# The first expert layer of a two-block kernel, cut into two half passes with other work beside each

## The chip, the cores and the metric

The kernel runs on one core of a Trainium2 chip, as one launch. The metric is the device time of a launch in microseconds (us). Five engines work side by side, each with its own queue of instructions: PE (TensorE, matrix multiplications and transposes), DVE (VectorE), ACT (ScalarE), POOL (GpSimd) and SP (SyncE, which here only starts transfers). The page calls a loading of stationary operands for a matmul PEld. Transfers between the chip's main memory and its on-chip memory are DMAs, carried by 16 DMA engines. Instructions of different engines wait for each other through semaphores; within one engine they run in the order in which they stand.

## The reference

The input is x, 4 batches of 512 tokens with 256 features, and a context of 4 batches of 1601 rows with 256 features. All arithmetic is in 32-bit floating point. Four blocks follow each other, and each adds its result to x:

```
x = x + attention_0(context, layernorm(x))   # 8 heads of 128, keys from the context and the tokens
x = x + experts_0(layernorm(x))              # 8 experts, 2 per token, limited room
x = x + attention_1(context, x)              # 8 heads of 32, queries from x, keys from the context
x = x + experts_1(layernorm(x))              # 8 experts, 2 per token, no limit
```

The change concerns the second block and the borders around it. A router gives each of the 2048 tokens a softmax over 8 experts, of which the two largest are taken. Each expert has room for 512 entries (the capacity is 2 x 2048 / 8). Entries are numbered in the order of the tokens, so that batch 0 fills the first places of every expert, then batch 1 and so on; an entry beyond 512 is dropped. Expert e computes, for its 512 places,

```
h = gelu(xb[e] @ w1[e])      # 512 x 256 by 256 x 1024, gelu in its tanh form
y = h @ w2[e]                # 512 x 1024 by 1024 x 256
```

and a token adds its two results, each multiplied by its softmax weight, and a bias. The third block then computes queries from the layernormed tokens, keys and values from the context, and a softmax with the row maximum taken away.

## The kernel before

**Stages.** The kernel has four parts after each other. The first attention handles 4 batches x 8 heads x 4 tiles of 128 queries; in its tail TensorE multiplies weights with values (`ps_o`, L829) and DVE adds the projected tile to x (L850). Each tile's weights pass through transfers (`swapped<-attn`) and a transpose on DVE (L821), and these transfers stand in SP's and ACT's queues. The routing of a batch (`route`) runs inside the attention of the next batch; only the last batch's is left for the second part. Instructions outside the parts with a written order are placed by a scheduler that goes by dependences and buffers; inside `in_order(...)` they stand as the program lists them. The second attention is such a part, from its first maxima on.

**Routing.** `route` gives three steps. `normalize` makes the layernorm `xn` of the batch and lets POOL add the bias to x. `choose` transposes `xn` (L163), multiplies by the router's weights (`ps_l`, L246), and DVE works out the two experts of each token and, with two small matmuls (`ps_c`, L285 and L288), each token's place, written as integers to `slot` (L298). A running count per expert is kept in `taken`. `send` lets POOL scatter the rows of `xn` to their places in a table in main memory, `slot_x` (L304), eight scatters of 128 rows.

**Experts.** `w_next` is the pair of weight matrices loaded ahead (L978, L979, one megabyte each). For each expert, SP loads its 512 rows from `slot_x` (`sx`, L1101), TensorE transposes them (L163), `expert` makes the hidden layer in blocks of 128 x 512 (L1041) with gelu on ACT (L1083), and `results` of the expert before multiplies by the second weights (L1054, blocks of 128 x 256), copies on DVE (L1088) and writes to `slot_y` in main memory (L1089). Between the experts SP issues up to six of 41 row clears (L385): transfers that fill two tables of the fourth block with zeros and a mark, about 540 KB each.

**Keys and values.** `keys_values(b)` loads the transposed context of batch b (L991), and makes keys (`ps_k1`, L1000) and values (`ps_v1`, L1016) of the second attention. ACT and DVE take turns to copy the results out (L109, L111). Those of batches 0 and 1 are made in the second part, before the experts: keys(0) beside the last batch's routing, keys(1) beside its scatters.

**Into the second attention.** POOL gathers the results of batch 0 from `slot_y` (L323, eight gathers), DVE adds them to x (L340), then follow a layernorm and transposes, the queries (`ps_q`, L1162), and per unit of 256 queries and 4 heads the scores (`ps_s`, L1216), their maxima on DVE (L1227, seven steps of two reductions), `negated` (L1236) and `to_row` (L1249, L1253). `keyed` is a table whose rows are filled with a constant (L1143, ACT, whole) and then loaded with the keys (L1182). `asked` takes queries and maxima (L1192). The weights (`ps_w`, L1266) of unit 0 follow.

The lines of the expert loop around which the order turns:

```
        normalize()
        kvs = [run(keys_values(ps_h, "h", 0))]
        choose()
        send()
        kvs.append(run(keys_values(ps_h, "h", 1)))
```

Of the kernel before, what the change touches and what calls it, by code (L numbers as in the profile page):

```python
# [43 lines left out]
CT = CAP // P  # L44
# [25 lines left out]
def xattn_ffn_twice(ctx: ExitStack, tc: tile.TileContext, a: dict, out: bass.AP):  # L70
# [143 lines left out]
    nc.vector.memset(taken, 0.0)  # L214
    prob = [const.tile([P, NX], F32, name=f"prob{k}") for k in range(2)]
# [4 lines left out]
    def route(b, rt, psum, tag):  # L220


        xn = rt.tile([P, NT, D], F32, tag="xn", name="xn")
# [16 lines left out]
        def choose():  # L240
            xnT = rt.tile([P, DC, S], F32, tag="xnT", name="xnT")
# [38 lines left out]
            for t in range(NT):  # L280
                nc.vector.tensor_copy(earlier[:, t, :], taken)
                nc.vector.tensor_tensor(taken, taken, cnt[:, t, :], ALU.add)
            ps = psum.tile([P, NT, E], F32, tag=tag, name="ps_c")
# [258 lines left out]
    with ExitStack() as st:  # L542
        w = st.enter_context(tc.tile_pool(name="a_w", bufs=1))
        one = st.enter_context(tc.tile_pool(name="a_one", bufs=1))
        rt = st.enter_context(tc.tile_pool(name="a_rt", bufs=1))
# [15 lines left out]
        kvin = one.tile([P, DC, NB, 4, 32], F32, name="kvin")  # L561
# [7 lines left out]
        def load_ctx(b):  # L569
            t = one.tile([P, NM, D], F32, tag="ctx", name="ctx_b")  # L570
            full = (NM - 1) * P
            nc.sync.dma_start(
                t[:, : NM - 1, :], a["ctx"][b, :full, :].rearrange("(t p) d -> p t d", p=P)
            )
            nc.sync.dma_start(t[:TAIL, NM - 1, :], a["ctx"][b, full:, :])
            return t
# [3 lines left out]
        wo = w.tile([P, H0, D], F32, name="wo")  # L580
# [3 lines left out]
        ctx_b = one.tile([P, NM, D], F32, tag="ctx", name="ctx_b")  # L584
# [27 lines left out]
        def keys_input(b, ctx_b):  # L612
# [9 lines left out]
            def latents():  # L622
                state["lat"] = lat = one.tile([P, NT, D], F32, tag="lat", name="lat")
                layernorm(two, lat, x[b], NT)
# [253 lines left out]
        scrap = one.tile([P, NT, D], F32, tag="lat", name="scrap")  # L878
# [15 lines left out]
        for n in range(n_steps + 4):  # L894
            b, h, t = n // (H0 * NT), n // NT % H0, n % NT
            if n < n_steps:
# [26 lines left out]
                if h == 1 and t == 1 and b > 0:  # L923
                    for k, f in enumerate(route(b - 1, rt, ps_t, "t")):
                        later[n + k].append(f)
# [109 lines left out]
    def expert(psum, pool, xT, w1, act):  # L1035

        hT = pool.tile([P, FC, 512], F32, tag="hT", name="hT")
        for f in range(FC):
            ps = psum.tile([P, 512], F32, tag="h", name="ps_h")
            for c in range(DC):  # L1040
                nc.tensor.matmul(  # L1041
                    ps,
                    lhsT=w1[:, c, f * P : (f + 1) * P],
                    rhs=xT[:, c, :],
                    start=c == 0,
                    stop=c == DC - 1,
                )
            act(hT[:, f, :], ps, f)
        return hT

    def expert_out(psum, hT, w2, t):
        ps = psum.tile([P, D], F32, tag="y", name="ps_y")
        for f in range(FC):
            nc.tensor.matmul(  # L1054
                ps,
                lhsT=hT[:, f, t * P : (t + 1) * P],
                rhs=w2[:, f, :],
                start=f == 0,
                stop=f == FC - 1,
            )  # L1060
        return ps


    with ExitStack() as st:
        two = st.enter_context(tc.tile_pool(name="b_two", bufs=2))
        rt = st.enter_context(tc.tile_pool(name="b_rt", bufs=1))
        ps_h = st.enter_context(tc.tile_pool(name="b_ps_h", bufs=3, space=PSUM))
        ps_y = st.enter_context(tc.tile_pool(name="b_ps_y", bufs=2, space=PSUM))
        ps_t = st.enter_context(tc.tile_pool(name="b_ps_t", bufs=2, space=PSUM))

        wexp = st.enter_context(tc.tile_pool(name="b_wexp", bufs=2))
        w_next = expert_weights(wexp, "w1", "w2", 0)


        normalize, choose, send = route(B - 1, rt, ps_t, "t")
        normalize()
        kvs = [run(keys_values(ps_h, "h", 0))]
        choose()
        send()
        kvs.append(run(keys_values(ps_h, "h", 1)))  # L1080

        def gelu_tanh(dst, ps, f):
            nc.scalar.activation(dst, ps, AF.Gelu_apprx_tanh)  # L1083

        def results(e, hT, w2):
            y = two.tile([P, CT, D], F32, tag="y", name="y")
            for t in range(CT):
                nc.vector.tensor_copy(y[:, t, :], expert_out(ps_y, hT, w2, t))  # L1088
            nc.sync.dma_start(  # L1089
                slot_y[e * CAP : (e + 1) * CAP, :].rearrange("(t p) d -> p t d", p=P), y  # L1090
            )

        empty = rt.tile([P, PAY], F32, name="empty")
        nc.gpsimd.memset(empty, 0.0)
        nc.gpsimd.memset(empty[:, D : D + 1], NOWHERE)
        clear = clear_rows(empty)
        last = None
        for e in range(E):
            w1, w2 = w_next
            sx = two.tile([P, CT, D], F32, tag="sx", name="sx")  # L1100
            nc.sync.dma_start(  # L1101
                sx, slot_x[e * CAP : (e + 1) * CAP, :].rearrange("(t p) d -> p t d", p=P)
            )
            sxT = two.tile([P, DC, CAP], F32, tag="xT", name="sxT")
            transposed(ps_t, "t", sxT, sx, CT)
            hT = expert(ps_h, two, sxT, w1, gelu_tanh)
            if last:
                results(*last)
            last = (e, hT, w2)
            if e + 1 < E:  # L1110
                w_next = expert_weights(wexp, "w1", "w2", e + 1)
                for _ in range(6):
                    next(clear, None)
        results(*last)
        assert next(clear, None) is None

        got0, steps = collect(0)
        for f in steps:
            f()
# [6 lines left out]
    QH = 2 * P  # L1126
    with ExitStack() as st:
# [5 lines left out]
        ps_m = st.enter_context(tc.tile_pool(name="c_ps_m", bufs=1, space=PSUM))  # L1133

# [3 lines left out]
        asked = [one.tile([P, 2, QH], F32, name=f"asked{i}") for i in range(3)]  # L1138
        shift = [one.tile([P, 2, 2, P], F32, name=f"shift{i}") for i in range(2)]
        for t in shift + asked:  # L1140
            nc.vector.memset(t, 0.0)
        for t in keyed:
            nc.scalar.activation(  # L1143
                t, ones[:, 0:1].unsqueeze(1).to_broadcast([P, 2, M]), AF.Copy, scale=in_row[:, 0:1]
            )

        def queries(b, qT):
            xn = one.tile([P, NT, D], F32, tag="xn", name="xn")
            mv = ln_moments(two, x[b], NT)
            root = ln_root(two, mv, NT)  # L1150
            yield
            mv, rs = ln_scale(two, mv, NT, root)
            for i in range(NT):
                ln_apply(xn, x[b], mv, rs, i)
            yield
            xnT = one.tile([P, DC, S], F32, tag="xnT", name="xnT")
            transposed(ps_s, "s", xnT, xn, NT)
            yield
            for o in range(DC):
                ps = ps_s.tile([P, 512], F32, tag="s", name="ps_q1")  # L1160
                for c in range(DC):
                    nc.tensor.matmul(  # L1162
                        ps,
                        lhsT=wT[:, 0, c, o * P : (o + 1) * P],
                        rhs=xnT[:, c, :],
                        start=c == 0,
                        stop=c == DC - 1,
                    )
                nc.scalar.activation(qT[:, o, :], ps, AF.Copy, scale=DH1**-0.5)
                yield  # L1170

        units = []
        for b in range(B):
            order = [(o, f) for o in range(DC) for f in range(2)]
            units += [(b, o, f) for o, f in order]
        qTs = {}
# [9 lines left out]

        def load_queries(u):
            b, o, f = units[u]
            for pair in range(2):
                for s in range(2):  # L1190
                    i = 2 * pair + s
                    nc.sync.dma_start(  # L1192
                        asked[u % 3][64 * s : 64 * s + 32, pair, :],
                        qTs[b][i * DH1 : (i + 1) * DH1, o, f * QH : (f + 1) * QH],
                    )


        rest = M // 512 * 512
        pieces = [[(t, j0, 512)] for t in range(2) for j0 in range(0, rest, 512)]
        pieces.append([(t, rest, M - rest) for t in range(2)])  # L1200
        assert 2 * (M - rest) <= 512
        n_tops = rest // 512 + 1
        tops = {}

        def maxima(u, g):

            b, o, f = units[u]
            if g == 0:
# [651 lines left out]
```

## Time and profile before

| what | us |
|---|---|
| median of 3 runs (2965.93 to 2965.98) | 2965.96 |
| the profiled execution | 2966.02 |
| its span | 2964.2 |
| last tile of x added by the first attention, at | 1602.8 |
| experts' matmuls begin, at | 1675.0 |
| experts' matmuls end, at | 1904.1 |
| first block of weights of the second attention, at | 1949.5 |

| engine | busy us | share of the span |
|---|---|---|
| PE | 2782.5 | 94% |
| DVE | 1458.7 | 49% |
| ACT | 942.5 | 32% |
| POOL | 391.9 | 13% |

The span is the time from the first to the last instruction in the profile; the rest of the profiled execution's time lies around it. A busy share is an average over four parts with different limits, so the prediction reads stretches of time instead. In the rows of groups, the number after the `|` is the sum of busy time, then the mean of one instruction in nanoseconds, then the idle time of the engine before these instructions and what ended most of it. A name such as L1054 is a line of the kernel's program; helpers have one line for all their callers. In the timeline the columns are start, duration, engine, line, operation, tiles, count, and in brackets the idle time before it with what ended it.

### The profile page before, as it was taken

The numbers are of one execution on the slowest core, as the hardware profiler recorded it, in microseconds if no ns is written. First come the engines' busy times: TensorE is split into PE (matmuls) and PEld (weight loads), VectorE is DVE, ScalarE is ACT, GpSimd is POOL, SyncE is SP. The second block draws the span as 40 slices with busy tenths as digits, with TensorE's granted clock in tenths as the row PEclk, the third lists the DMA queues.
The fourth block names the chain that finished last, engine by engine and source line by source line (L and its number), as shares of the span: only waits on it lengthen the run. The fifth ranks groups of instructions, "written<-read, shape, count | busy, mean of one in ns | idle before, by whom it ended". The sixth has DMA issues, their size and how long they took to land. (4 is left out here: it accounts for less than half of the span.)

```text
span 2964.2 us, 35563 instructions
## 1 busy us (share of the span) xinstructions
PE 2782.5 (94%) x13426; PEld 1841.3 (62%) x13426; DVE 1458.7 (49%) x2333; ACT 942.5 (32%) x1330; POOL 391.9 (13%) x301
## 2 busy tenths in 40 slices
PE   6999999999999999999997999788989898889997
PEld 3666667666766666666665566544454444468886
DVE  6445456454575444454444100267877768742110
ACT  4323234332343233333321212124434344341221
POOL 0000000100001000010000100121314233233442
PEclk9999999999999999999998999879999999899999
DMA  5434443334434333343336379310101022035553
GB/s 164 113 104 112 106 113 89 102 95 103 109 88 109 97 95 91 87 111 97 87 93 177 103 191 234 100 27 14 31 27 47 18 66 65 11 109 156 178 186 86
DMA packets 184512, 295.96 MB, mean 100 GB/s; under 512 B 43367, under 2 KB 107176, under 8 KB 181512
## 3 DMA queue, kind: packets, MB, share of 16 engines
q1 hardware_dynamic: 144584, 208.64, 26.8%
q0 software_dynamic: 15168, 49.23, 5.6%
q10 hardware_dynamic: 24576, 35.68, 4.6%
q8 instruction: 109, 1.79, 0.3%
q14 instruction: 75, 0.61, 0.1%
HBM read 97.86 MB, written 49.76 MB: 50 GB/s over the span
## 5 line engine op out<-in xcount | busy, mean ns | idle before, releaser
L800 DVE TENSOR_REDUCE top<-ps_s 128x1 f32<-128x2113 f32 x128 | 301.7, 2357 | 579.7 <-PE ps_s L792 579.7
L829 PE MATMUL ps_o<-pT,v 128*128 128x256 f32 x2176 | 521.6, 381 | 7.7 <-DVE pT L821 7.7
L792 PE MATMUL ps_s<-kT,qT 128*128 128x512 f32 (+1 forms) x1280 | 488.9, 526 | 4.7 <-ACT attn L806 4.7
L829 PEld LDWEIGHTS ps_o<-pT,v 128*128 128x128 f32 x2176 | 409.8, 191 | 122.3 <-issue 68.4
L806 ACT ACTIVATE attn<-ps_s,top 128x2113 f32<-128x2113 f32 x128 | 259.0, 2024 | 476.0 <-DVE top L800 430.5
L792 PEld LDWEIGHTS ps_s<-kT,qT 128*128 128x128 f32 x1280 | 241.6, 190 | 251.0 <-issue 236.8
L821 DVE STREAM_TRANSPOSE pT<-swapped 128x2176 f32<-128x2176 f32 x128 | 312.4, 2441 | 34.4 <-DMA swapped<-attn 24.2
L1227 DVE TENSOR_REDUCE tops<-ps_s 128x2 f32<-128x1024 f32 (+1 forms) x224 | 237.4, 1104 | 141.1 <-PE ps_s L1216 140.8
L741 PE MATMUL ps_k<-kvin,wkv 128*128 128x512 f32 (+1 forms) x640 | 263.6, 535 | 4.1 <-DVE mv_g L679 2.1
L1266 PE MATMUL ps_w<-asked,keyed 64*128 64x256 f32 (+1 forms) x1664 | 246.6, 418 | 20.2 <-DVE tops L1227 9.5
L775 PE MATMUL ps_v<-wkv,kvin 128*128 128x256 f32 x1088 | 254.4, 381 | 0.0
L1279 ACT ACTIVATE pT<-ps_w 128x1024 f32<-128x1024 f32 (+1 forms) x176 | 179.5, 1024 | 195.2 <-PE ps_w L1266 191.5
L1266 PEld LDWEIGHTS ps_w<-asked,keyed 64*128 64x128 f32 (+1 forms) x1664 | 148.7, 191 | 145.4 <-ACT pT L1279 61.8
L775 PEld LDWEIGHTS ps_v<-wkv,kvin 128*128 128x128 f32 x1088 | 204.9, 190 | 34.7 <-ACT v L782 4.5
L1288 DVE TENSOR_TENSOR sum<-sum,pT 128x1024 f32<-128x1024 f32 (+1 forms) x128 | 182.7, 1428 | 10.7 <-ACT pT L1279 4.0
L754 ACT ACTIVATE kT<-ps_k,bqk 128x512 f32<-128x512 f32 (+1 forms) x160 | 97.0, 620 | 264.7 <-DMA swapped<-attn 123.8
L1288 POOL TENSOR_TENSOR sum<-sum,pT 128x1024 f32<-128x1024 f32 x48 | 122.6, 2555 | 347.4 <-ACT pT L1279 347.2
L741 PEld LDWEIGHTS ps_k<-kvin,wkv 128*128 128x128 f32 x640 | 116.2, 192 | 78.6 <-issue 68.0
L1216 PE MATMUL ps_s<-kv,qT 32*128 32x512 f32 (+1 forms) x1024 | 143.4, 594 | 12.2 <-ACT kv L1007 6.5
L782 ACT COPY v<-ps_v 128x512 f32<-128x512 f32 x144 | 79.8, 561 | 216.4 <-PE ps_v L775 140.9
L1054 PE MATMUL ps_y<-w,hT 128*128 128x256 f32 x512 | 112.8, 379 | 0.0
L1041 PE MATMUL ps_h<-sxT,w 128*128 128x512 f32 x256 | 111.8, 594 | 0.5 <-issue 0.4
(275 smaller groups left out, 2684.2 us busy)
## 6 DMA issues: line engine op xcount, KB each, us to landing
swapped<-attn SPq DMA_DIRECT2D x1536, 68.0 KB, 2.0
swapped<-attn ACTq DMA_DIRECT2D x512, 68.0 KB, 2.3
rows_b<-empty SPq DMA_DIRECT2D x36, 530.0 KB, 11.6
w<-in_w_dram SPq DMA_DIRECT2D x16, 1024.0 KB, 6.3
w_e<-in_wall_dram SPq DMA_DIRECT2D x4, 2052.0 KB
cw<-in_ctxT_dram SPq DMA_DIRECT2D x4, 1601.0 KB, 6.7
keyed<-kv SPq DMA_DIRECT2D x32, 200.1 KB, 3.4
ctx_b<-in_ctx_dram SPq DMA_DIRECT2D x3, 1536.0 KB
```

Of the source, the lines that this page charges most:

```text
L741: nc.tensor.matmul(ps[:, :n], lhsT=wkv[:, c, hs], rhs=kvin[:, c, : NB - 1, k, :] if k < 4 else kvin[:, c, NB - 1, :, :], start=c == 0, sto ...
L775: nc.tensor.matmul(ps[:, k, :], lhsT=flat_kvin[c][:, j * P : (j + 1) * P], rhs=wkv[:, c, cols], start=c == 0, stop=c == DC - 1,)
L792: nc.tensor.matmul(flat[:, j0 : j0 + n], lhsT=qT[:, t * P : (t + 1) * P], rhs=kT[:, j0 : j0 + n], start=True, stop=True,)
L800: nc.vector.tensor_reduce(top, flat[:, :L], AX.X, ALU.max, negate=True)
L806: nc.scalar.activation(attn[:, :L], flat[:, :L], AF.Exp, bias=top, accum_out=total)
L821: nc.vector.transpose(pT[:, :, k * P : (k + 1) * P].rearrange("p c (a i) -> p a c i", a=4), swapped.rearrange("p a (c i) -> p a c i", i=32),)
L829: nc.tensor.matmul(ps, lhsT=v[:, j - parts[part][0], (h % 2) * DH0 : (h % 2 + 1) * DH0], rhs=pT[:, j, :], start=j == 0, stop=j == NB - 1,)
L1216: nc.tensor.matmul(pss[i // 2][:, i % 2, at : at + n], lhsT=qTs[b][rows, o, q0 : q0 + P], rhs=kvs[b][0][o][rows, j0 : j0 + n], start=True, ...
L1227: nc.vector.tensor_reduce(tops[u][:, t : t + at // n, 2 * pair : 2 * pair + 2, j0 // 512], of, AX.X, ALU.max,)
L1266: nc.tensor.matmul(ps[:r, s, pair * QH : (pair + 1) * QH], lhsT=keyed[o][64 * s : 64 * s + 64, pair, j * P : j * P + r], rhs=asked[u % 3][ ...
L1279: nc.scalar.activation(pT[:r], ps[:r], AF.Exp)
L1288: (nc.gpsimd if k else nc.vector).tensor_tensor(to, to, pT[:r], ALU.add)
```

## The change

The experts' 512 places are cut into a lower and an upper half of 256. `all_experts(half, beside)` runs one half of all 8 experts, in the order transposes, hidden layer, results of the expert before, and takes two steps of a generator of other work per expert.

- In the first pass the other work is `keys_first`: the last batch's normalize, choose, send, and keys(0). The first loads, `fetched(0, 0)`, do not depend on the last batch's routing. Rows, weights and results have two buffers each; the weights are loaded for each half, so twice in all.
- In the second pass it is `keys_next`: keys(1), the adds of batch 0's gathered results, the queries of batch 0, all maxima of unit 0, `negated` and `to_row`. The gathers of batch 0 stand between the passes.
- The first pass is enough for batch 0's results, and independent of the last batch, when no expert has more than 256 entries from batch 0 and every expert has at least 256 from batches 0 to 2. `route` notes both counts in `reached`. Between the passes DVE tests them, the engines load the value (`values_load`), and a branch (`tc.If`) computes all 16 halves again for other counts.
- The hidden layer is made in blocks of 256 columns, two of them in one bank of the accumulators, with one gelu for both; results of 256 places share one bank and one copy.
- `clears` puts 8 transfers ahead of the row clears, which fill the upper half of each expert's part of `slot_y` with zeros; four transfers are issued per expert in place of six.
- The filling of `keyed` is split between ACT and DVE; the zeroing of `asked` and `shift` moves ahead of the expert layer.
- For the maxima of unit 1, the first three steps stand ahead of the loop.
- Tiles of the first attention change their pools (sides of the on-chip memory), so that the new pools find room.

```diff
@@ route @@
+            if b in (0, B - 2):
+                nc.vector.tensor_copy(reached[:, int(b > 0), :], taken)
@@ the second part @@
-        w_next = expert_weights(wexp, "w1", "w2", 0)
-        normalize, choose, send = route(B - 1, rt, ps_t, "t")
-        normalize()
-        kvs = [run(keys_values(ps_h, "h", 0))]
-        choose()
-        send()
-        kvs.append(run(keys_values(ps_h, "h", 1)))
...
+        def fetched(e, half):
+            sx = two.tile([P, CT, D], F32, tag="sx", name="sx")
+            nc.sync.dma_start(sx, slots(slot_x, e, half))
+            w1 = two.tile([P, DC, FF], F32, tag="w1", name="w1")
+            w2 = two.tile([P, FC, D], F32, tag="w2", name="w2")
+            nc.sync.dma_start(w1, a["w1"][e].rearrange("(c p) f -> p c f", p=P))
+            nc.sync.dma_start(w2, a["w2"][e].rearrange("(c p) d -> p c d", p=P))
+            return e, half, sx, w1, w2
...
+        def all_experts(half, beside):
+            here = turned(*fetched(0, half))
+            last = None
+            for e in range(E):
+                done = hidden(*here)
+                next(beside, None)
+                for _ in range(4):
+                    next(clear, None)
+                if e + 1 < E:
+                    here = turned(*fetched(e + 1, half))
+                if last:
+                    results(*last)
+                next(beside, None)
+                last = done
+            results(*last)
...
+        def clears():
+            for e in range(E):
+                tc.keep_in_program_order(
+                    nc.sync.dma_start(
+                        slots(slot_y, e, 1), empty[:, :D].unsqueeze(1).to_broadcast([P, CT, D])
+                    )
+                )
+                yield
+            yield from clear_rows(empty)
...
+        def keys_first():
+            normalize()
+            yield
+            choose()
+            send()
+            yield
+            *kv, steps = keys_values(ps_s, "s", 0)
+            kvs.append(kv)
+            for k, f in enumerate(steps):
+                f()
+                if k % 2:
+                    yield
+
+        normalize, choose, send = route(B - 1, rt, soon, ps_t, "m")
+        all_experts(0, keys_first())
+        ps = ps_t.tile([P, 2, E], F32, tag="m", name="ps_r")
+        for k in range(2):
+            nc.tensor.matmul(ps[:, k, :], lhsT=ones, rhs=reached[:, k, :], start=True, stop=True)
+        odd = rt.tile([P, 2, E], F32, name="odd")
+        nc.vector.tensor_scalar(odd[:, 0, :], ps[:, 0, :], float(HALF), None, ALU.is_gt)
+        nc.vector.tensor_scalar(odd[:, 1, :], ps[:, 1, :], float(HALF), None, ALU.is_lt)
...
+        again = nc.values_load(odds_i[0:1, 0:1], min_val=0, max_val=2 * E)
+        with tc.If(again > 0):
+            for half in range(2):
+                for e in range(E):
+                    results(*hidden(*turned(*fetched(e, half))))
 
         got0, steps = collect(0)
         for f in steps:
             f()
+        def keys_next():
+            *kv, steps = keys_values(ps_s, "s", 1)
+            kvs.append(kv)
+            for f in steps[:6]:
+                f()
+            yield
+            add_collected(0, got0)
+            for k, f in enumerate(steps[6:]):
+                f()
+                if k % 3 == 2:
+                    yield
+            begin(0)
+            for _ in queries(0, qTs[0]):
+                yield
+            load_queries(0)
+            for g in range(len(pieces)):
+                maxima(0, g)
+                yield
+            negated(0)
+            to_row(0)
+
+        all_experts(1, keys_next())
@@ the second attention @@
         for t in keyed:
-            nc.scalar.activation(
-                t, ones[:, 0:1].unsqueeze(1).to_broadcast([P, 2, M]), AF.Copy, scale=in_row[:, 0:1]
-            )
+            nc.scalar.activation(t[:, 0], of_ones, AF.Copy, scale=in_row[:, 0:1])
+            nc.vector.tensor_scalar(t[:, 1], of_ones, in_row[:, 0:1], None, ALU.mult)
...
-        for g in range(len(pieces)):
-            maxima(0, g)
-        negated(0)
-        to_row(0)
+        for g in range(3):
+            maxima(1, g)
```

## The prediction

> **What bounds the kernel now.** I read the page first, then busy time by stretch between the two attentions, then the waits there, then the timeline. The page prices an expert's matmuls:
>
> ```profile
> L1054 PE MATMUL ps_y<-w,hT 128*128 128x256 f32 x512 | 112.8, 379 | 0.0
> L1041 PE MATMUL ps_h<-sxT,w 128*128 128x512 f32 x256 | 111.8, 594 | 0.5 <-issue 0.4
> rows_b<-empty SPq DMA_DIRECT2D x36, 530.0 KB, 11.6
> ```
>
> Neither group waits (0.0 and 0.5 us). The row clears are the other load here: half a megabyte each, all issued beside the experts.
>
> Busy time by stretch; the columns are length, PE (instructions), PEld, DVE, ACT, POOL, granted clock, DMA share, GB/s:
>
> ```profile
> 1602.00:1617.00 15.00, 6.30 (x24) 4.93 (x24) 8.62 (x32) 3.36 (x4) 3.39 (x6) 0.62 1.01 366
> 1617.00:1643.00 26.00, 25.60 (x88) 16.58 (x88) 9.06 (x34) 3.97 (x8) 0.00 (x0) 0.89 0.67 167
> 1643.00:1650.00 7.00, 0.80 (x2) 0.50 (x2) 1.82 (x12) 0.00 (x0) 0.99 (x1) 0.76 0.69 246
> 1650.00:1675.00 25.00, 24.85 (x92) 16.30 (x90) 4.57 (x8) 4.11 (x8) 6.85 (x7) 0.93 0.19 62
> 1675.00:1904.00 229.00, 228.52 (x826) 151.05 (x824) 18.50 (x39) 44.19 (x73) 0.00 (x0) 1.00 0.69 174
> 1904.00:1932.00 28.00, 7.26 (x17) 3.57 (x16) 11.21 (x33) 8.49 (x6) 8.04 (x8) 0.63 0.36 100
> 1932.00:1949.00 17.00, 14.41 (x69) 6.17 (x68) 14.56 (x16) 0.76 (x2) 0.00 (x0) 0.74 0.20 47
> ```
>
> The experts (1675 to 1904) are TensorE-bound: 228.5 of 229 us at full clock. Around them TensorE idles 8.7 us beside the last batch's layernorm, 6.2 before the second keys, 20.7 at the end, at clocks of 0.62 to 0.76 (the 20.7 while the gathers, 1908 to 1918, the adds and a layernorm run); and from 1932 its matmuls are paced by DVE's maxima (14.56 of 17).
>
> The waits between 1595 and 1975 (sum, times, longest):
>
> ```profile
> POOL slot_x L304 <- DVE at L295: 31.9, 1, 31.9
> PE tp L163 <- issue: 28.5, 2, 20.6
> SPq L1101 <- DMA slot_x<-xn,slot: 26.7, 1, 26.7
> ```
>
> The experts' first rows wait for the scatters, which wait for the slots. The timeline has the marks I count from:
>
> ```profile
> 1644.62 0.99 POOL L304 DMA_INDIRECT slot_x<-xn,slot  x1 [31.90 <-DVE at L295]
> ...
> 1667.58 0.98 POOL L304 DMA_INDIRECT slot_x<-xn,slot  x1 [1.54 <-DMA slot_x<-xn,slot]
> ...
> 1907.59 5.82 ACT L1143 ACTIVATE keyed<-ones,in_row 128x3202 f32<-128x3202 f32 x2 [30.05 <-DMA slot_y<-y]
> ...
> 1924.70 2.04 PE L163 MATMUL tp<-ident,xn 128*128 128x128 f32 x8 [20.59 <-issue]
> ...
> 1954.11 9.15 DVE L1227 TENSOR_REDUCE tops<-ps_s 128x2 f32<-128x1024 f32 x8 [6.35 <-PE ps_s L1216]
> ```
>
> The last query tile is added at 1602.8; the second unit's first four steps of maxima end at 1963.3 (1954.11 + 9.15). From there on both kernels have one order of work. So the change plays between these marks, 360.4 us, plus whatever it does to the tail of the first attention.
>
> **The Trainium skill.** "TensorE: Matmul & The Clock Gate", Part 1, says that TensorE falls to half clock after about an idle window of 3.4 us and needs as long a busy one to recover. The trace agrees: clocks of 0.5 to 0.67 after each hole, a 128x512 instruction 0.85 us there against 0.427. "DMA: Bandwidth & Descriptors", "Issuing engines are not separate DMA queues", says all queues share 16 DMA engines and interleave; share 1.01 at 1602 to 1617 shows that state. "Runtime: NRT & Kernel Launch", "Instruction fetch mechanics", says that a taken branch to a target outside the fetch window waits for a DMA of instructions. Before's trace shows such a branch only at the very end (L1742): 45 to 72 ns on four engines, 3.36 us on TensorE, 2.4 of it while its matmuls still ran.
>
> **The branch.** It redoes all 16 halves if, by expert, batch 0 fills over 256 slots or batches 0 to 2 fewer than 256. I worked the routing out from the reference on its inputs: at most 167 and at least 264. It isn't taken, so the body costs only the jump over it.
>
> **The change, part by part.**
>
> *Nothing less to multiply.* Half an expert is 16 + 16 logical matmuls of 256 columns at 0.43 us plus 4 transposes (0.67 for all): 14.4 us, half of before's 28.64. Sixteen are 230, as before.
>
> *First halves begin early.* In the built order, hidden(0) and five sixteenths of results(0) stand before the last output blocks of the first attention, where TensorE is idle 7.7 us (1582.4 to 1590.1): 9 us of work, about 7 hidden. Hidden(1), results(0) and (1) and all of keys(0) surround the routing. The price: their loads sx(0), w1(0), w2(0), 2.4 MB, sit on SP ahead of an exchange about four tiles from the end; at the 390 to 410 GB/s of weight loads that is up to 6 us late, and the exchange waits in that tail are only 0.2 to 4.3 us. Some falls into the refilled hole. I take 3 us (0 to 6): last tile 1605.8.
>
> *Routing to scatters.* Before: 6.9 us to the first transposes, 6.9 for transposes and logits, 7.5 of DVE chain, then 18 us because ps_c stood behind keys(0). Now ps_c stands in the middle of keys(0); I give 2.5 for ps_c and slots. ACT takes gelus and five memsets of 0.51 us stand on DVE: 2 us more. 1605.8 + 8.9 + 6.9 + 7.5 + 2.5 = 1631.6. Eight scatters, 22.9 us from first to last start before, make it 1654.9; SP then issued the rows 2.5 us later and the transposes came 4.1 after that: sx(2) at 1661.5, or 1659.7 without the two scatters which a context load stretched. I take 1659.7. TensorE's filler (about 48 us from 1605.8, 2 more for clock) ends near 1656: a stall of some 4 us, up to 12. That stall is the new wait: tp(2) on sx(2), with ctxT(1) and the later weights queued behind it on SP.
>
> *First pass, rest.* 1.2 us for transpose and copy, six halves at 14.32 = 86, 2 for the clock: 89.2. DMA here: 5.3 us weights, 0.9 rows, 0.9 results, and four clears. Two rates:
>
> ```profile
> 1844.00:1846.00 2.00, 2.00 (x6) 0.83 (x5) 0.00 (x0) 0.60 (x1) 0.00 (x0) 1.00 1.12 235
> 1613.00:1615.00 2.00, 1.85 (x10) 1.75 (x9) 0.36 (x1) 0.91 (x1) 0.00 (x0) 0.50 1.01 410
> ```
>
> Clears run at 235 GB/s (2.3 us each), weights at 410. With four row clears a half needs 16.3 us of DMA against 14.4 of TensorE: 1.9 late times six is 11, less the lead of two weight buffers. I take 3 (0 to 11).
>
> *Branch.* ps_r and its DVE chain stand ahead of the last results, hidden. The loads of the value (0.5 us per engine in before's last lines), the semaphores (9 of 50 ns) and the jump: 3 us (1 to 8, the upper end with a full fetch and drained engines). Pass ends 1605.8 to 1659.7 + 89.2 + 3 + 3 = 1754.9.
>
> *Second pass.* 8 x 14.32 = 114.6; keys(1) 22.2 less 3.5 matmul pairs done, 19; queries and transposes 4.5 warm; maxima(0) 7 on TensorE, DVE's 15.4 us now hidden beside 50 us of matmuls; 4 because keys(1)'s copies on DVE stand behind adds that wait for the gathers (8 x 1.3). 149.1: ends 1904.0. Weights are the same 5.3 us per half, and hidden (6 clears' rest too, since TensorE has 35 us more).
>
> *Into the attention.* y copy 0.7, the write 3.0 (keyed waits for it, as at 1907.59), keyed halved over two engines 3.4, eight reduces 9.15: 16.3. Ends 1920.3 against 1963.3: **43.0 us gained**. Cross-check by TensorE's work from 1605.8 to 1904.0 (298 us): experts 230, keys 44, routing 7, queries and maxima 11.5, less 9 done before: 283.5; waits 4 + 2 + 3 + 3 + 4: 299.5. What leaves the path is mainly the idle 8.7, 6.2, 7.7 and 20.7 and the slow, paced stretch up to 1949.
>
> The profiled execution took 2966.02 (span 2964.2), the median is 2965.96: 2966.0 - 43.0 = **2923.0**.
>
> **Rivals.**
> *Waits hidden.* Exchange delay, DMA lag and copy delay at 0, branch 1, layernorm undisturbed: 14 us better (3 + 3 + 4 + 2 + 2), 17 if keyed does not wait for the write: 2906 to 2909. For it: TensorE has slack holes there. Against: SP works without a pause through that tail.
> *DMA is the bound in the first pass.* 11 instead of 3, exchange 6, stall 12: 2966 - 43 + 8 + 3 + 8 = 2942, and 2951 with a branch of 8 and copies of 8. For it: clears now come beside twice the weight traffic. Against: before's 36 clears with 6 weight loads cost DMA share 0.69 x 229 = 158 us, near the 142 that my prices give.
> *Slower: weights at the clears' rate.* With both kinds in flight, each weight load might get only what clears get: 2.1 MB at 235 GB/s is 8.9 us, four clears 9.2, rows and results 1.8, 19.9 per half, 5.5 late over 12 halves: 66 lost, 2989. It decides from 14.4 + 43/12 = 18 us of DMA per half. Against: the shares just summed.
> *The branch is taken after all* (counts wrong): 16 halves without overlap at 18 to 20 us: 3210.
> *The change does nothing*: only if the holes reappear whole elsewhere; I see no mechanism.
>
> **How the numbers follow.** My forecast, 2911 to 2935: 0.62. Hidden waits: 0.13. DMA bound, 2935 to 2951: 0.18. Weights at clear rate: 0.05. Branch taken: 0.01. No change: 0.01. 0.2% (6 us) is about what can be told from none. The range 2904 to 2948 takes in the hidden case and most of the DMA one. Faster 0.93, same 0.01, slower 0.06.
>
> **What would show it.** After: slots before 1635; last scatter before 1658; one TensorE stall at tp(2) of 2 to 12 us; halves of 14.3 to 14.6 us in the first pass (16 and more means DMA); a hole of 1 to 8 us near 1750 at the branch; no hole at gathers; the first reduce after keyed near 1911; the last tile of the first attention 0 to 6 us late. A first-pass half above 18 us, or instructions of the branch body in the trace, would make me wrong in sign.

## The result, and the profile after

The changed kernel takes 2953.05 us (median of 7 runs, 2946.82 to 2959.16) against 2965.98 us (7 runs, 2961.55 to 2967.73). The ratio is 0.9955, with a 95% interval of 0.9942 to 0.9967. It is faster, by 13 us where 43 were forecast, and the time lies 5 us above the range. The profiled execution took 2949.11 us (span 2947.0), 16.9 less than the profiled one of before; the accounts below are made on it, so they explain 17 of what varies from run to run around 13.

The page of the changed kernel, the rows that answer to those of before:

```profile
L1193 PE MATMUL ps_h<-sxT,w 128*128 128x256 f32 x512 | 116.7, 386 | 2.9 <-ACT hT L1200 2.1
L1207 PE MATMUL ps_y<-w,hT 128*128 128x256 f32 x512 | 114.4, 380 | 0.2 <-DVE y L1215 0.2
...
w<-in_w_dram SPq DMA_DIRECT2D x32, 1024.0 KB, 10.2
rows_b<-empty SPq DMA_DIRECT2D x36, 530.0 KB, 11.3
```

The multiplications, now in halves, cost 231.1 us against 224.6. There are 32 weight loads in place of 16, and the median one lands after 10.2 us and not 6.3.

Busy time by stretch (length, PE, PEld, DVE, ACT, POOL, granted clock, DMA share, GB/s):

```profile
1612.00:1656.00 44.00, 43.18 (x190) 32.48 (x189) 21.29 (x77) 10.40 (x16) 4.95 (x6) 1.00 0.88 246
1656.00:1678.00 22.00, 1.33 (x7) 0.71 (x6) 0.23 (x1) 1.87 (x2) 5.87 (x6) 0.61 0.32 84
1678.00:1769.00 91.00, 90.22 (x415) 78.22 (x416) 8.08 (x15) 14.33 (x24) 0.00 (x0) 0.96 1.00 255
1769.00:1776.00 7.00, 3.72 (x10) 1.49 (x9) 1.38 (x2) 0.58 (x1) 2.11 (x3) 1.00 0.22 72
1776.00:1909.00 133.00, 130.87 (x602) 105.32 (x602) 33.26 (x57) 25.86 (x43) 5.93 (x6) 0.97 0.80 228
1930.00:1945.00 15.00, 11.26 (x54) 5.06 (x52) 11.45 (x11) 6.97 (x6) 0.75 (x1) 0.77 0.45 109
```

The holes of before (layernorm, second keys, gathers and queries) are gone: TensorE works 43.2 of 44 us beside the routing and 131 of 133 beside gathers, queries and maxima. But one stretch of 22 us has 1.3 us of matmuls, and before it the DMA engines are 88% busy.

The waits of the same stretch of time:

```profile
POOL slot_x L308 <- DMA slot_x<-xn,slot: 27.8, 7, 10.6
PE tp_x L1183 <- DMA sx<-slot_x: 20.7, 1, 20.7
PE ps_k L1006 <- PEq L1282: 3.3, 1, 3.3
```

TensorE waits once, 20.7 us, for the rows of the third half expert (a stall of 4 was forecast), and 3.3 at the branch. GpSimd's scatters wait 27.8 us in sum for each other, against 16.1 before:

```profile
POOL slot_x L304 <- DMA slot_x<-xn,slot: 16.1, 7, 4.5
```

The timeline of the changed kernel shows what stands beside them:

```profile
1631.96 4.63 SPq L389 DMA_DIRECT2D rows_a<-empty  x4
...
1638.07 0.99 POOL L308 DMA_INDIRECT slot_x<-xn,slot  x1 [15.03 <-ACT kv L112]
...
1644.99 6.79 SPq L389 DMA_DIRECT2D rows_b<-empty  x4
...
1649.64 0.98 POOL L308 DMA_INDIRECT slot_x<-xn,slot  x1 [10.58 <-DMA slot_x<-xn,slot]
...
1657.87 0.98 POOL L308 DMA_INDIRECT slot_x<-xn,slot  x1 [7.25 <-DMA slot_x<-xn,slot]
...
1672.74 0.98 POOL L308 DMA_INDIRECT slot_x<-xn,slot  x1 [1.55 <-DMA slot_x<-xn,slot]
...
1677.89 1.12 PE L1183 MATMUL tp_x<-ident,sx 128*128 128x128 f32 x4 [20.67 <-DMA sx<-slot_x]
```

SP issues eight row clears, 4.2 MB, right around the first scatters. The first three scatters then take 11.6, 8.2 and 4.6 us from start to the next start, and the rest 2.6 us, as most did before. The DMA share is 1.02 to 1.12 from 1638 to 1658, beside the first two, 0.41 beside the third and 0.09 beside the others. The transposes of the third half follow 5 us after the last scatter starts.

The marks of the prediction:

| mark | before | predicted | after |
|---|---|---|---|
| last tile of x complete | 1602.8 | 1605.8 | 1612.1 |
| places written | 1644.3 | 1631.6 | 1637.2 |
| last scatter starts | 1667.6 | 1654.9 | 1672.7 |
| third half's transposes | | 1659.7 | 1677.9 |
| branch passed | | 1754.9 | 1775.7 |
| second pass ends | | 1904.0 | 1927.0 |
| eight reductions end | 1963.3 | 1920.3 | 1943.7 |

At the last mark 19.6 us are gained, 23.4 fewer than forecast: 18.2 of them are lost before the third half's transposes, the other 5.2 in four small pieces after it. From that mark to the end of the span it is 1000.9 us before and 1003.3 after; these 2.4 us are not explained.

### The profile page after: what moved, and what is told of

It reads as the page before. It is cut to its first block, busy times and chain, and to the rows that moved or that the text cites. A ratio compares the mean times of both kernels' runs of the same rounds, so it can differ in the third digit from the quotient of the medians.

```text
span 2947.0 us, 36216 instructions
## 1 busy us (share of the span) xinstructions
PE 2770.3 (94%) x13686; PEld 1883.4 (64%) x13686; DVE 1466.2 (50%) x2333; ACT 937.7 (32%) x1325; POOL 392.5 (13%) x301
## 5 line engine op out<-in xcount | busy, mean ns | idle before, releaser
L1109 PE MATMUL ps_s<-kv,qT 32*128 32x512 f32 (+1 forms) x1024 | 135.4, 574 | 14.6 <-ACT kv L1013 6.5
L1193 PE MATMUL ps_h<-sxT,w 128*128 128x256 f32 x512 | 116.7, 386 | 2.9 <-ACT hT L1200 2.1
## 6 DMA issues: line engine op xcount, KB each, us to landing
w<-in_w_dram SPq DMA_DIRECT2D x32, 1024.0 KB, 10.2
```

Source lines behind the costliest of these rows:

```text
L1109: nc.tensor.matmul(pss[i // 2][:, i % 2, at : at + n], lhsT=qTs[b][rows, o, q0 : q0 + P], rhs=kvs[b][0][o][rows, j0 : j0 + n], start=True, ...
```

## The experiments

Theory A, mine after the result: the clears' traffic stretches the scatters, and the rows' wait for the last scatter turns that into idle TensorE. Rival B: the scatters are slowed by something else. Theory C: the loss comes from the tail of the first attention, where the first half's loads stand ahead of the exchanges.

**Clears later in the layer.**

```diff
-                for _ in range(4):
+                for _ in range(0 if half == 0 and e < 3 else 4):
                     next(clear, None)
```

> The changed kernel without clears beside its first three half experts (none there, four from the fourth on; the last ones fall in the second pass). Theory A, clears slow the scatters by sharing the DMA engines, and the experts' rows wait for the last scatter: first to last scatter start 23 to 27 us instead of 34.7, TensorE's stall before the third half's transposes 9 to 13 us instead of 20.7, time about 2943 (2939 to 2947) against the changed kernel's 2953. Rival B, the scatters are slowed by weight and context loads or by something on GpSimd itself: 32 to 36 us, time within 3 us of 2953.

Measured: 2948.37 us (ratio 0.9952, 0.9933 to 0.997). From the first scatter's start to the last's it is 22.9 us (1638.68 to 1661.53), the third half's transposes come at 1666.7. Its waits:

```profile
POOL slot_x L308 <- DMA slot_x<-xn,slot: 16.0, 7, 5.8
PE tp_x L1183 <- DMA sx<-slot_x: 9.7, 1, 9.7
PE ps_h L1193 <- DMA w<-in_w_dram: 8.0, 1, 8.0
```

Scatters and stall are as theory A had them, and B falls. The median is 1 us outside A's interval: in the second pass, where most of the clears now are, a half's matmuls wait 8.0 us for weights (at 1883). The scatters gave 11 us, and the layer kept 5. One scatter still took 6.7 us, beside a weight load and the zeroing of `slot_y` (a DMA share of 0.91), so it need not be a row clear that stretches one.

**Rows ahead of the scatters.**

```diff
             normalize()
             yield
+            for e in range(2, E):
+                sx = rt.tile([P, CT, D], F32, name=f"sx{e}")
+                tc.keep_in_program_order(nc.sync.dma_start(sx, slots(slot_x, e, 0)))
+                ahead_rows.append(sx)
             choose()
             send()
```

`fetched` takes its rows from this list while there are any.

> The changed kernel with the rows of half experts 2 to 7 loaded into buffers of their own before the last batch's scatters are issued, so that no load of rows waits for them; the clears stay. If the wait of the third half's transposes for its rows is what holds the path: the stall of 20.7 us falls to 3 or less, time about 2935 (2931 to 2940). Rival, the same transfers are then late in another place (the weights of the third half behind the clears): a stall of 10 us or more on weights, time 2945 to 2953.

Measured: 2938.32 us (0.9906, 0.9888 to 0.9924). Its waits:

```profile
POOL slot_x L308 <- DMA slot_x<-xn,slot: 38.0, 6, 9.4
...
PE ps_k L1006 <- PEq L1291: 7.0, 1, 7.0
```

The scatters now take 53.6 us (1640.89 to 1694.45), and nothing on TensorE waits for them: the stall is gone. They are stretched more than in the changed kernel, and it costs TensorE no wait, since nothing stands behind them. What remains is a hole of 7.0 us at the branch, 3.7 longer than in the changed kernel. SP is not late there: it passes its own branch instruction at 1751.2, 2 us before TensorE. TensorE's branch instruction itself takes 7.06 us, against 3.89 in the changed kernel, and the DMA share beside it is 0.75, against 0.13. That fits the prediction's reading of such a branch, which waits for a transfer of instructions; no run tests this alone.

**First loads held behind the exchanges.** The three transfers of `fetched(0, 0)` are kept in program order.

```diff
+            load = tc.keep_in_program_order if (e, half) == (0, 0) else lambda i: i
...
-            nc.sync.dma_start(sx, slots(slot_x, e, half))
+            load(nc.sync.dma_start(sx, slots(slot_x, e, half)))
```

(and the same for both weights)

> The changed kernel with the first half's three loads kept behind the first attention's last exchanges on SP. Theory C, these loads delay the exchanges and the half expert's matmuls stand in front of the last output blocks: x's last tile back from 1612 to about 1603, everything to the scatters 9 us earlier, the stall about 11 instead of 20.7 since nine us of matmuls move behind the tile, time about 2944 (2940 to 2948). Rival, the tail is late for another reason (the moved pools): x's last tile stays near 1610, time 2953 within 3.

Measured: 2972.62 us (1.0026, 1.0017 to 1.0036), slower than before. x's last tile is 5.3 us earlier, at 1606.8. But the half expert's matmuls now stand within the routing, so the scatters start at 1642.0, 4 us later than in the changed kernel, and the build placed 26 of keys(0)'s 52 value instructions and 16 of its key instructions after the transposes that stall. The stretch from these transposes (1678.8) to the matmuls behind the branch (1791.8) grew from 98 to 113 us, 3.7 of this in the hole at the branch. Both theories missed: it isn't a test of the tail alone, since the order moved with it. The early half expert together with the order that goes with it is worth 20 us; the two weren't separated.

**Without the branch.**

```diff
-        again = nc.values_load(odds_i[0:1, 0:1], min_val=0, max_val=2 * E)
-        with tc.If(again > 0):
-            for half in range(2):
-                for e in range(E):
-                    results(*hidden(*turned(*fetched(e, half))))
```

> The changed kernel without the load of the counts' test and without the branch and its body (the test's arithmetic stays; these inputs don't take the branch). If the branch costs its visible hole: 3 to 5 us less, 2949 (2946 to 2951). Rival, the hole is covered elsewhere or the order changes with it: within 2 us of 2953.

Measured: 2964.34 us (0.9999, 0.999 to 1.0007), 11 us worse than with it. Its waits between 1740 and 1960:

```profile
POOL g L327 <- DMA rows_b<-empty: 118.8, 1, 118.8
...
DVE x L344 <- DMA g<-slot_y,slot: 22.2, 2, 21.0
```

The gathers come at 1793.4 and not 1773.3. Without the branch the build lets SP issue second-pass rows and weights, and clears, among the first pass's last weights and writes of results. The last results of the first pass wait 5.7 us for their weights (until 1769.2), and their writes follow later still. DVE's adds then wait 21 us for gathers, with keys(1)'s copies behind them, and TensorE waits 14.4 us for such a copy. The branch had kept the second pass's transfers out of the first.

**Clears into the attention, and with it rows ahead.** The clears are taken out of the generator of the layer and spread over 41 steps of the second attention:

```diff
-            yield from clear_rows(empty)
...
+        row_clears = clear_rows(empty)
+        spread(8, row_clears, 1, 41)
```

> The changed kernel with its 41 row clears issued in the first steps of the second attention, where the DMA engines are nearly idle; the eight clears of the results' upper halves stay. If the clears' traffic costs the layer its gain in both passes: first to last scatter 23 to 25 us, a stall of 9 to 11 us, no wait for weights in the second pass (the 8.0 us that came up when clears were only pushed later in the layer), time about 2941 (2937 to 2945) against 2953. Rival, the clears hold up the attention's own transfers of keys and queries there: 2948 or more.

> The clears in the attention as in the run beside it, and the rows of half experts 2 to 7 loaded ahead of the last batch's scatters. If the two losses add: no stall, a hole at the branch of 3 to 4 us and not 7 (SP has no clears queued there), time about 2931 (2927 to 2935). Rival, with the rows early the weights bind: waits on weights of 5 us or more in the first pass, 2936 or more.

Measured: 2949.56 us (0.9944, 0.9925 to 0.9963) and 2931.86 us (0.9886, 0.9869 to 0.9902). The first missed; its time is the rival's, but not for the rival's reason, and its trace says why: SP is not held to the written order in the attention, so the build pulled these clears up into the second pass (19 of them before its last weights), where the last results waited 7.3 us for weights. The second run did as expected, with the same flaw; its waits:

```profile
PE ps_y L1212 <- DMA w<-in_w_dram: 7.2, 1, 7.2
...
PE ps_k L1006 <- PEq L1290: 3.3, 1, 3.3
```

The hole at the branch is back at 3.3 us, and the DMA share beside TensorE's branch instruction at 0.15: no clears are in flight there now.

**First weights from GpSimd's queue** (on top of the last), and in **the kernel before, two one-megabyte copies** at the place of the changed kernel's first weights:

```diff
+            by = nc.gpsimd if (e, half, bool(kvs)) == (0, 0, False) else nc.sync
...
+                if n == n_steps - 4:
+                    for name in ("w1", "w2"):
+                        tc.keep_in_program_order(nc.sync.dma_start(
+                            dram.tile([D, FF], F32, name=f"copy_{name}"), a[name][0]...))
                 swapped = exchange(attn)
```

> The run with both edits, and the first half expert's two weight loads issued by GpSimd in place of SP; the second half expert's weights then stand ahead of the last four exchanges on SP, by the order that the build makes. If a queue of its own lets the exchanges through between the weights' packets: x's last tile near 1607 in place of 1611 to 1614, time 3 to 5 us below the run without it. Rival, the same engines carry the same bytes at that time and as much again: no gain, within 3 us or worse.

> The kernel before, with two copies of one megabyte each (main memory to main memory, of no use) at the place on SP's queue where the changed kernel has its first weights: ahead of the first attention's fourth-last exchange. Theory C, they delay the exchanges of a tail without slack: x's last tile at 1607 to 1610 in place of 1602.8, everything after it by as much, time about 2971 (2969 to 2974). Rival, the tail has slack: the tile and the time within 2 us of before's.

Measured: 2938.18 us (0.9912, 0.9893 to 0.9931), x's last tile at 1614.5: no gain from another queue, and 6 us more than without it. And 2967.04 us (1.0002, 0.9993 to 1.0011): no difference. There x's last tile comes 1.6 us later, and 1.4 of this was there before the copies were issued (the 124th of the attention's maxima starts at 1532.6 against 1531.2). So 2 MB at that place cost the exchanges nothing measurable; the copies were through before the next exchange began. They ran at 524 GB/s, though, and the changed kernel's loads at 370, up to the start of the exchange.

**Clears really out of the layer.** They read a block that GpSimd fills in the attention, so that they can't be moved up. Once in the changed kernel, once with the rows ahead, and once in the kernel before.

```diff
+        blank = one.tile([P, PAY], F32, name="blank")
+        def fill():
+            nc.gpsimd.memset(blank, 0.0)
+            nc.gpsimd.memset(blank[:, D : D + 1], NOWHERE)
+        put(8, fill)
+        row_clears = clear_rows(blank)
+        spread(9, row_clears, 1, 41)
```

> The changed kernel with the 41 row clears kept out of the layer altogether: they read a block of zeros that GpSimd fills only in the second attention, so the build can't move them into the second pass, as it did in the run with clears in the attention (there the last weights waited 7.3 us). If the clears' bytes are what both passes lack: scatters 21 us, stall near 6, no wait for weights, the gathers' gain of 16 us kept to the end of the layer: about 2938 (2934 to 2942). Rival, they cost the attention what they cost the layer: 2946 or more.

> The same, with the rows of half experts 2 to 7 loaded ahead of the scatters. If waits for DMA were all that stood between the estimate and the measurement: no stall, no wait for weights at the end of the second pass (7.2 us in the run with both edits, 2931.9), time about 2924 (2920 to 2928), which is the time predicted for the change. Rival, another wait takes their place: 2930 or more.

> The kernel before with the same move of its 41 row clears into the second attention. If they cost nothing there because whole experts leave the DMA engines room, and cost nothing in the attention: within 2 us of before's 2965. Rival, they also delayed something before (rows or weights): 2961 or less; or they cost in the attention: 2968 or more.

Measured: 2936.20 us (0.9897, 0.9879 to 0.9916); 2923.61 us (0.9854, 0.9837 to 0.987); and for before 2969.57 us (1.0005, 0.9996 to 1.0014). The clears cost the changed kernel 17 us and the kernel before nothing that can be told: its median without them is 3 us higher, in the rival's range, but the interval of the ratio takes in no change. In the first of these runs the eight scatters take 22.6 us, as the prediction had it, and still the third half's transposes wait 8.5 us for their rows and come at 1668.2, where 1659.7 was forecast: the first scatter starts late, at 1640.5. Rows ahead take this wait away, and are worth another 13 us. Busy time of the version with both:

```profile
1613.00:1657.00 44.00, 43.26 (x207) 35.45 (x206) 22.20 (x82) 11.62 (x18) 8.30 (x11) 1.00 0.71 240
1657.00:1749.00 92.00, 91.69 (x415) 76.13 (x413) 10.02 (x19) 14.29 (x24) 2.93 (x3) 1.00 0.37 125
1749.00:1905.00 156.00, 148.95 (x702) 120.13 (x702) 37.29 (x65) 27.06 (x45) 8.05 (x8) 0.98 0.46 153
```

TensorE works 91.7 of 92 us where the changed kernel stalled, and the DMA share of both passes is 0.37 and 0.46, not 1.00 and 0.80. This version beats both kernels and keeps the branch. That its time is the predicted 2923.0 is in part chance (see the sum below).

**The same without the branch** (it then serves only inputs that would not take it):

> The last version (row clears out of the layer, rows ahead) without the load of the test's value, the branch and its body. In the changed kernel, taking the branch out let SP issue clears and second-pass loads ahead of the first pass's last write of results, and the gathers came 20 us later; with the clears gone there is little left to pull forward. If so, only the hole goes: 3 to 4 us below 2923.6, about 2920 (2918 to 2922). Rival, the branch is worth more as a fence than it costs: gathers later than at 1755 us and a time of 2926 or more.

Measured: 2921.11 us (0.9851, 0.9831 to 0.9872), 2.5 us less, with intervals that overlap. It is no longer a loss. The hole of 3.6 us went, but a wait of 5.5 us of TensorE for one of keys(1)'s copies came, so the branch's own price isn't measured closer than that.

## Why the prediction was wrong

**What held.** The branch isn't taken and costs 3.3 us (3 forecast). From x's last tile to the places it took 25.1 us (25.8). TensorE's other work beside the routing ended at 1657 (1656). The second pass took 151.3 us (149.1), and the step into the attention 16.7 (16.3), with `keyed` behind the last write as written. The holes of before did leave the path. The cover that I named for queries, maxima and gathers held: TensorE works 131 of 133 us beside them.

**The term that failed: "Eight scatters, 22.9 us from first to last start before, make it 1654.9."** They took 34.7. I carried over a duration from a stretch with a DMA share of 0.19, into one where the change puts clears and weight loads, at a share of 1.02 to 1.12. The trace of before had the sign: the first scatter took 5.5 us, beside a context load at a share of 0.70. I saw it and used it the other way, taking 1.8 us off for "the two scatters which a context load stretched" (the other one, of 4.6 us, had no load beside it: a share of 0.06). I had the clears' bytes in the sum, but only against the weights of each half ("1.9 late times six is 11"). That lag did not come: the transposes of the last three halves of the pass follow each other every 14.25 us, at a DMA share of 1.00. The bytes took their price where a chain of eight small transfers, each waiting for the one before, had to share the engines. The Trainium skill's "DMA: Bandwidth & Descriptors", "Issuing engines are not separate DMA queues", which I had quoted, says that transfers started by different engines run on the same 16 DMA engines and interleave; here the scatters are GpSimd's and the clears SP's. What that costs, the traces show: 11.6, 8.2 and 4.6 us for the first three scatters, which share with clears and weight loads, 2.6 for the others; and 22.9 and 22.6 us for all eight in the two runs that only kept the row clears away from them.

**The stall.** "A stall of some 4 us, up to 12" became 20.7, by these 11.8 us and the late tile. The wait itself was named and priced by its place ("that stall is the new wait"), only its size was off.

**The tail.** I took 3 us (0 to 6) for the first attention's last tile, and it came 9.3 late. Of these 3.7 were there at the 124th maxima (1534.9 against 1531.2), ahead of anything that the change issues. The profiles of the changed kernel and its variants have this mark between 1532.7 and 1537.6, three of the kernel before and its variants between 1531.2 and 1532.6; so some of it seems to belong to the change, of which only the moved pools act that early. That wasn't tested. Then the last transposes are 3.7 later still, and the last output blocks start 4.7 us after these end, since matmuls of the half expert stand in front of them. First before, then the changed kernel:

```profile
1587.58 2.45 DVE L821 STREAM_TRANSPOSE pT<-swapped 128x2176 f32<-128x2176 f32 x1 [4.29 <-DMA swapped<-attn]
...
1590.08 10.24 PE L829 MATMUL ps_o<-pT,v 128*128 128x256 f32 x34 [7.71 <-DVE pT L821]
```

```profile
1594.97 2.44 DVE L827 STREAM_TRANSPOSE pT<-swapped 128x2176 f32<-128x2176 f32 x1 [0.19 <-issue]
...
1599.93 2.32 PE L1207 MATMUL ps_y<-w,hT 128*128 128x256 f32 x10
...
1602.09 7.50 PE L835 MATMUL ps_o<-pT,v 128*128 128x256 f32 x34
```

At full clock they run 2.7 us faster than before (a granted clock of 1.00 against 0.73), which makes 9.4. I had said that 7 of the 9 us would be hidden, and had not priced the 2 that weren't, nor the wait that the order makes when the transposes come first. My cause for the rest, loads in front of exchanges, is not borne out by the copies in the kernel before. In the changed kernel DVE also takes the next maxima ahead of a transpose (1567.29 and 1569.57) where before the transpose came first (1561.15 and 1563.57). In the run that held the first loads back the order is that of before again, and the last transposes start 56.2 us after the 124th maxima, as before (56.4, against 60.0 in the changed kernel). So this second piece of 3.7 us comes with the early loads or with this order, not with the pools; which of the two stays open. That the half expert and its loads together make the tail late is shown by the same run: there the mark is 5.3 us later than before, and the last tile only 4.0. In the changed kernel the late tile counts, with 6.3 us more than forecast ahead of scatters that the rows wait for. With no wait behind it, it decides little: the version that reaches 2923.6 has its last tile at 1614.2, and a late tile then shifts work of TensorE that must be done in any case.

**The rivals.** "DMA is the bound in the first pass" (2942 to 2951, 0.18) named the cause and the wrong victim: it charged 8 us for halves that lag, which they did not, and 8 for a longer stall, which grew by 17. Its chance was too small, and the range too narrow above, because I took the clears for a matter of average rates. Weights at the clears' rate did not happen.

**Sum.** Clears out gives 17 us and rows ahead 13: together 29.4 of the 30 us by which the median missed. These two edits thus take out as much time as was missed, but that the sum fits is in part chance: rows ahead also take away a wait of which the forecast itself counted 4 us, and x's last tile is still 8 us later than forecast. What the runs show is that the clears' traffic and the rows' wait for the last scatter cost these 29 us; how they divide between the stretched scatters, the late tile and the slower parts after the stall is only read from the traces (some 12, 6 and 5 us of the 23.4).

## What to carry to other kernels

When work is pulled forward beside a serial chain of small transfers, price the chain again with the traffic that now runs beside it; a duration from a quiet stretch does not carry over. Bulk transfers that cost nothing beside a compute-bound loop must find a new home when that loop's loads double, and pushing them later in the same loop only moves the wait: put them where the DMA engines idle. And look at who waits for the end of the chain: loading rows that don't depend on it ahead of it was worth 13 to 15 us, where making the chain faster by pushing the clears later was worth 5.

## What the runs showed of the hardware

- A scatter of 128 rows of 1 KB, from its start to the next one's, took 2.6 us at a DMA share of 0.09, 5.4 to 6.0 us beside weight loads at 0.62 to 0.76 (the version with clears out and rows ahead), and 11.6 us beside 530 KB clears from another queue and a weight load at 1.07. Eight of them stretched from 22.9 to 53.6 us with weights and clears in flight beside most of them.
- Jumping over the branch's body costs TensorE 2.9 to 3.7 us where the DMA share beside it is 0.11 to 0.15, and 7.0 us where it is 0.75 and 0.97. Between two stretches of work it is also a fence: taking it out cost 11 us in one version and nothing in another.
- Executions of the changed kernel differ by 12 us from fastest to slowest of 7, those of before by 6 (8 among 22 on another chip). The marks in the first attention alone spread over 5 us; the cause was not looked for.
